# A local transformer on one core: values projected in every step, attention as keys by queries on eight tiles, the output weights gathered in one PSUM bank, and the feed-forward norm folded into W1

## The chip, the core and the metric

The kernel runs on one core of a Trainium2 chip. The core has a matrix engine (PE; its weight loads are listed as PEld), a vector engine (DVE), a scalar engine (ACT), a general engine (POOL) and a queue that issues most DMAs (SP). Each engine works through its own list of instructions in order; semaphores tie the lists together. Matrix products land in PSUM, which has eight banks of 128 partitions by 2 KB. The metric is the device time of one execution in microseconds (us), the median of several runs.

## The reference

All of it is float32. The batch is 16 sequences of 256 tokens, 128 channels. Layer 0 applies a linear-attention block and then a six-layer local transformer; layer 1 applies a causal attention with position bias and a feed-forward block. The change touches the local transformer alone:

```python
# DEPTH 6, HEADS 16, DIM_HEAD 64, WINDOW 32, DIM_INNER 341
for i in range(DEPTH):
    x = attn_layer(shift_tokens(x), Wqkv[i], q_scale[i], k_scale[i], Wo[i]) + x
    x = ffn_layer(shift_tokens(x), ln_g[i], ln_b[i], W1[i], b1[i], W2[i], b2[i]) + x

def attn_layer(x, Wqkv, qs, ksc, Wo):
    q, k, v = heads(x @ Wqkv)
    q, k = rotary(l2norm(q) * qs), rotary(l2norm(k) * ksc)
    # each window of 32 queries sees its own 32 keys and the 32 before
    sim = where(mask, -max, (q @ k_two_windows.T) * 8.0)
    return concat_heads(softmax(sim) @ v_two_windows) @ Wo

def ffn_layer(x, g, bln, W1, b1, W2, b2):
    xn = (x - mean(x)) / sqrt(var(x) + 1e-05) * g + bln
    a, gate = split(xn @ W1 + b1)
    return a * gelu(gate) @ W2 + b2
```

`shift_tokens` takes the second half of the channels from the token before.

## The kernel before

The state is kept channels by tokens, in eight tiles `zs[u]`, one for each unit of 512 tokens (two sequences). The local transformer works layer by layer, unit by unit, and in a unit over four steps; a step `n` handles two pairs of heads, that is four heads. There are 6 x 8 x 4 = 192 steps, and the loop runs 16 more to drain, because a step's work is spread over the iterations after it (lines 1053 to 1137). Iteration `n` does, in the order in which it is written:

- scores, maxima and exponentials of step n-5 (lines 842, 855, 868). The 16 exponentials of an iteration are dealt out between later work by the generator `between`;
- the projection of queries and keys of step n (line 699), four products of 128x128 by 512 columns. ACT squares each bank (703), then DVE multiplies the same bank twice by the rotary tables (706, 709); halves of heads are exchanged by DMA (`sent`, `got`) and added by POOL an iteration later (`rotate`, 719);
- the norms of queries and keys in pairs of steps: sums of squares on PE (727), transposed (745), three Newton steps for the inverse root on POOL (763 to 771), turned into rows (779) which go to DRAM (`home`) and come back spread over partitions as `kn`, with which POOL scales the keys (800);
- the mask for the next scores, copied into PSUM by ACT (828);
- the probabilities of step n-6 are divided by their sums on POOL (889) and transposed in 32x32 blocks by DVE (896) into `prT`;
- attention with merged weights. `upright` (802) transposes the state, and a DMA pair shifts it by one window (`own`, `before`). `weighted` (901, step 910) multiplies the state itself by all 16 heads' probabilities of 128 tokens, in 8 products of 32x128 weights and 512 columns, four banks, copied to `zx` by ACT and DVE (919, 917). `merging` (922, step 927) multiplies that, head by head, by Wv times Wo of that head: 16 products of 128 columns, summed in one bank, and `merged_in` adds them to the state (940). The 16 matrices Wv Wo are made once a layer by `merge_vo` (653 to 680);
- the feed-forward block of a unit, 15 to 19 iterations after the unit's first step: mean by a product (956), square on ACT (961), variance by four one-column products (965), the power -0.5 on POOL (975) and its spreading (977), transposed back (981), the scaling by g and b (982, 983), the gates (990), the values (997), W2 (1007).

The order of PE, DVE, ACT and POOL is the written one (`manual_schedule`); DMA issues on SP are placed by the scheduler. Products land in `bank()`, a pool of five PSUM banks of 128x512; three more hold scores. A bank is handed out again when its last reader has been issued and done; which free bank a product gets goes by the order in which they are released.

Of the kernel before, what the change touches and what calls it, by code (L numbers as in the profile page):

```python
# [19 lines left out]
NU = B // 2  # L20
# [24 lines left out]
def adaln_kernel(  # L45
# [44 lines left out]
    nc.vector.memset(mean128, 1.0 / D)  # L90
    half = cst.tile([128, 16], F32, tag="half", name="half")
# [144 lines left out]
    with block:  # L236
# [17 lines left out]
        centre = wa.tile([128, 128], F32, tag="centre", name="centre")  # L254
        nc.vector.tensor_tensor(centre, ident, mean128, ALU.subtract)
# [342 lines left out]
    with ExitStack() as es:  # L598
        pss = psum(es, 5, 3)
# [26 lines left out]
        own = [persistent(f"own{j}", (128, 4, D)) for j in range(2)]  # L626
        before = [persistent(f"before{j}", (128, 4, D)) for j in range(2)]
# [25 lines left out]
        def merge_vo(i, vo):  # L653

            for g in range(2):
                wv = work("wv")
                c0 = 2 * INNER + g * 512
                nc.sync.dma_start(wv, io["L0_ffn_Wqkv"][i, :, c0 : c0 + 512])
                wo = work("wo").rearrange("p (j d) -> p j d", j=4)
                nc.sync.dma_start(  # L660
                    wo,
                    io["L0_ffn_Wo"][i, g * 512 : (g + 1) * 512, :].rearrange(
                        "(p k) d -> k p d", k=128
                    ),
                )
                yield
                pt = bank()
                for j in range(4):
                    c = slice(j * 128, (j + 1) * 128)
                    nc.tensor.transpose(pt[:, c], wv[:, c], ident)  # L670
                wt = work("wvT")
                nc.scalar.copy(wt, pt)
                yield
                for par in range(2):
                    r = slice(64 * par, 64 * par + 64)
                    pw = bank()
                    for j in range(4):
                        c = slice(j * 128, (j + 1) * 128)
                        nc.tensor.matmul(pw[:, c], wt[r, c], wo[r, j, :], start=True, stop=True)
                    nc.vector.tensor_copy(  # L680
                        vo[:, 8 * g + par : 8 * g + 8 : 2, :],
                        pw.rearrange("p (j d) -> p j d", j=4),
                    )
                yield

        def project(i, u, m, wqk, between):
# [3 lines left out]
            xs = zs[u][:, :, PAD : PAD + L]  # L690
            squares = []
            sent, got = atile("sent", (128, 2, 512)), atile("got", (128, 2, 512))
            q = two(atile("q", (128, 512), 10))
            k = ks[m % 10][:, :, PAD:]
            for j, (name, r) in enumerate((("q", q), ("k", k))):
                tab = [rope[:, j, a].unsqueeze(1).to_broadcast([128, 2, L]) for a in range(2)]
                scale = bcol(i, name + "s")
                pp = bank()
                nc.tensor.matmul(pp, wqk[:, j, :], xs, start=True, stop=True)  # L699
                sq = work("sq")  # L700
                first = False
                if not first:
                    nc.scalar.activation(sq, pp, AF.Square)  # L703
                squares.append(sq)
                next(between, None)
                nc.vector.scalar_tensor_tensor(  # L706
                    two(sent[:, j, :]), two(pp), scale, tab[1], ALU.mult, ALU.mult
                )
                nc.vector.scalar_tensor_tensor(r, two(pp), scale, tab[0], ALU.mult, ALU.mult)  # L709
                if first:  # L710
                    nc.scalar.activation(sq, pp, AF.Square)
# [895 lines left out]
```

## Time and profile before

| | |
|---|---|
| median of 3 runs | 3831.9 us (3828.32 to 3834.38) |
| the profiled execution | 3831.36 us, span 3829.5 us |
| local transformer in it, first projection to last state addition | 264.8 to 3284.6 us |
| PE busy, weight loads, DVE, ACT, POOL, share of the span | 94%, 58%, 74%, 72%, 69% |
| exponentials (L868), 3072 | 1248.7 us, and 755.3 us of accumulator reads |
| projections (L699), 768 products | 730.2 us |
| merging (L927), 3072 products | 718.2 us |
| weighting (L910), 1536 products | 524.6 us |
| scores (L842), 12288 products | 310.6 us |

A float32 product shows as two PE instructions with a weight load each, so the counts in the profile are twice the products. A row of the groups reads: line, engine, operation, output<-input, shapes, count | busy us, mean ns of one | idle time of the engine just before, and what released it. The times of one group overlap on PE, where instructions are pipelined: the mean of one is longer than busy time divided by count. A row of the timeline gives start, length, engine, line and the instructions that stand together.

### The profile page before, as it was taken

To read this page: it belongs to the slowest core of one execution; us is meant where nothing else is said; L and a number is where in the kernel's file an instruction comes from. 1 tells how busy PE (TensorE), PEld (TensorE's weight loads), DVE (VectorE), ACT (ScalarE), POOL (GpSimd) and SP (SyncE) were. 2 spreads that over 40 slices of the span, in tenths; PEclk is the share of its full clock that TensorE was granted. 3 is DMA by queue.
4 is the path that set the end of the run, shared out by engine and by line. 5 is a ranking of instruction groups with operands and counts; after the bars stand their busy time and mean duration, and the time that the engine had idled before them with its cause. 6 is when DMAs were issued, how large, how long until landed. Compare 5 with 4: busy or idle time off the path is not lost.

```text
span 3829.5 us, 120148 instructions
## 1 busy us (share of the span) xinstructions
PE 3597.0 (94%) x46454; PEld 2227.9 (58%) x46454; DVE 2846.2 (74%) x5941; ACT 2768.1 (72%) x9651; POOL 2657.0 (69%) x3380
## 2 busy tenths in 40 slices
PE   7875899999999999999999999999999999789888
PEld 4542566666666666666666666566666666355554
DVE  6745777777777777777777777777777774587774
ACT  4544787878878787777878787787778775366664
POOL 6536877777777777777777777777777772345453
PEclk9887999999999999999999999999999999799998
DMA  1324444544444444454444444444444440201000
GB/s 43 45 61 113 121 112 113 128 108 114 123 109 123 108 115 121 113 125 104 116 121 116 119 113 108 116 119 123 112 110 116 110 106 23 75 16 27 12 21 10
DMA packets 216210, 362.27 MB, mean 95 GB/s; under 512 B 63657, under 2 KB 107608, under 8 KB 215640
## 3 DMA queue, kind: packets, MB, share of 16 engines
q1 hardware_dynamic: 215640, 354.59, 37.6%
q8 instruction: 368, 6.03, 0.7%
q14 instruction: 202, 1.65, 0.1%
HBM read 132.12 MB, written 9.96 MB: 37 GB/s over the span
## 4 chain that ended last, share of the span: by engine, by line
PE 72%; DVE 9%; POOL 8%; ACT 6%; issue 4%; DMA 1%; SPq 1%; POOLq 0%; ACTq 0%; DVEq 0%
PE mm L699 15%; PE mm L927 14%; PE mm L910 9%; PE sim L842 7%; PE mm L727 5%; PE mm L990 3%; PE mm L997 3%; PE mm L1007 3%; POOL k L800 3%; ACT pr L1344 2%; DVE sent L706 2%; PE sim L1315 1%; PE mm L1404 1%; PE mm L956 1%; PE mm L1301 1%
## 5 line engine op out<-in xcount | busy, mean ns | idle before, releaser
L868 ACT ACTIVATE pr<-sim,nb,rq 128x64 f32<-128x64 f32 x3072 | 1248.7, 445 | 19.2 <-DVE nb L859 17.8
L927 PEld LDWEIGHTS mm<-zx,wvo 128*128 128x128 f32 x6144 | 716.5, 192 | 90.6 <-issue 80.3
L868 ACT ACTIVATION_READ_ACCUMULATOR pr<-sim,nb,rq 128x1 f32 x3072 | 755.3, 246 | 0.0
L699 PE MATMUL mm<-z,wqk 128*128 128x512 f32 x1536 | 730.2, 608 | 4.7 <-DMA wqk<-in_L_ffn_Wqkv_dram 4.6
L927 PE MATMUL mm<-zx,wvo 128*128 128x128 f32 x6144 | 718.2, 275 | 1.0 <-DVE zx L917 1.0
L703 ACT ACTIVATE sq<-mm 128x512 f32<-128x512 f32 x768 | 474.5, 618 | 317.5 <-PE mm L699 317.5
L706 DVE SCALAR_TENSOR_TENSOR sent<-mm,vec,rope 128x512 f32<-128x512 f32 x768 | 569.3, 741 | 160.1 <-ACT sq L703 130.8
L889 POOL TENSOR_TENSOR pr<-pr,rsum 128x512 f32<-128x512 f32 x384 | 392.2, 1042 | 419.7 <-DVE rsum L881 414.9
L719 POOL TENSOR_TENSOR q<-q,got 128x512 f32<-128x512 f32 x384 | 496.9, 1294 | 20.0 <-DMA got<-sent 12.5
L800 POOL TENSOR_TENSOR k<-k,kn 128x512 f32<-128x512 f32 x384 | 481.7, 1276 | 14.8 <-DMA kn<-rkh 14.8
L719 POOL TENSOR_TENSOR k<-k,got 128x512 f32<-128x512 f32 x384 | 489.1, 1274 | 0.0
L699 PEld LDWEIGHTS mm<-z,wqk 128*128 128x128 f32 x1536 | 275.7, 192 | 350.5 <-issue 269.6
L855 DVE TENSOR_REDUCE mx<-sim 128x8 f32<-128x512 f32 x384 | 246.6, 683 | 185.9 <-PE sim L842 183.9
L842 PE MATMUL sim<-k,q 64*32 64x64 f32 x24576 | 310.6, 228 | 69.6 <-POOL k L800 55.4
L842 PEld LDWEIGHTS sim<-k,q 64*32 64x32 f32 x24576 | 267.7, 107 | 173.7 <-POOL k L800 114.6
L1358 POOL TENSOR_TENSOR pr<-pr,rsum 128x256 f32<-128x256 f32 (+1 forms) x256 | 206.2, 836 | 221.7 <-DVE rsum L1356 221.5
L1344 ACT ACTIVATE pr<-lg,nm 128x128 f32<-128x128 f32 (+1 forms) x512 | 226.4, 443 | 128.9 <-DVE nm L1333 119.2
L917 DVE COPY zx<-mm 128x512 f32<-128x512 f32 x384 | 247.4, 686 | 67.1 <-PE mm L910 61.3
L709 DVE SCALAR_TENSOR_TENSOR k<-mm,vec,rope 128x512 f32<-128x512 f32 x384 | 284.9, 742 | 0.0
L709 DVE SCALAR_TENSOR_TENSOR q<-mm,vec,rope 128x512 f32<-128x512 f32 x384 | 284.6, 741 | 0.0
L919 ACT COPY zx<-mm 128x512 f32<-128x512 f32 x384 | 210.0, 610 | 99.2 <-PE mm L910 94.2
L910 PE MATMUL mm<-prT,before 32*128 32x512 f32 x1536 | 273.1, 636 | 0.6 <-ACT pr L868 0.6
(250 smaller groups left out, 5832.7 us busy)
## 6 DMA issues: line engine op xcount, KB each, us to landing
got<-sent SPq DMA_DIRECT2D x1536, 128.0 KB
kn<-rkh SPq DMA_DIRECT2D x768, 128.0 KB
before<-own SPq DMA_DIRECT2D x48, 192.0 KB
wqk<-in_L_ffn_Wqkv_dram SPq DMA_DIRECT2D x48, 128.0 KB
v<-vh SPq DMA_DIRECT2D x32, 128.0 KB
bhome<-brow SPq DMA_DIRECT2D x1, 3072.0 KB
wv<-in_L_ffn_Wqkv_dram SPq DMA_DIRECT2D x12, 256.0 KB
wo<-in_L_ffn_Wo_dram SPq DMA_DIRECT2D x12, 256.0 KB
```

What stands on the lines that cost most here:

```text
L699: nc.tensor.matmul(pp, wqk[:, j, :], xs, start=True, stop=True)
L703: nc.scalar.activation(sq, pp, AF.Square)
L706: nc.vector.scalar_tensor_tensor(two(sent[:, j, :]), two(pp), scale, tab[1], ALU.mult, ALU.mult)
L709: nc.vector.scalar_tensor_tensor(r, two(pp), scale, tab[0], ALU.mult, ALU.mult)
L719: nc.gpsimd.tensor_tensor(r, r, two(got[:, j, :]), ALU.add)
L800: nc.gpsimd.tensor_tensor(k, k, two(kn), ALU.mult)
L842: nc.tensor.matmul(sims[par][32 * c : 32 * c + 32, c0 : c0 + 64], q[r, s, t0 : t0 + 32], k[r, s, t0 : t0 + 64], start=False, stop=True, sk ...
L868: nc.scalar.activation(pr[:, x, st, par, :], sims[par][:, b * 64 : (b + 1) * 64], AF.Exp, bias=nb[:, par, b : b + 1], scale=rn[:, par, b : ...
L889: nc.gpsimd.tensor_tensor(prf, prf, rsum[:, x].unsqueeze(2).to_broadcast([128, 8, 64]), ALU.mult)
L910: nc.tensor.matmul(pz[c], xw[b][r, j, :], moving[r, j, b], start=(b == 0), stop=(b == 1))
L927: nc.tensor.matmul(py, vo[:, h, :], zx[:, h % 2, h // 2, :], start=(h == 0), stop=(h == 2 * NP - 1),)
L1344: nc.scalar.activation(pr[:, par, SPANS[t]], lg[:, par, SPANS[t]], AF.Exp, bias=nm[:, t, par : par + 1], scale=-1.0, accum_out=ssum[:, t, ...
```

## The change

- **Values.** `merge_vo`, `upright`, `weighted`, `merging` and `merged_in` go. Each step projects its own four heads' values for the unit (`values`, V0 and V1, one for each sequence): four products with the state as weights and 256 columns of Wv, copied to `v` by ACT.
- **Probabilities.** `pr` is laid out by window first (o=0 the earlier 32 keys, o=1 the own 32). `divided` and `flipped` work on one half at a time (D0, D1, F0, F1). The transposed earlier half goes to `prB` and by two DMAs, shifted by one window, beside the own half in `prT`: so each block of 32 keys stands by the 32 queries of its own window and the 32 of the next one.
- **Attention.** `attended` (A) multiplies, for two head pairs, four token tiles, four key blocks and two heads, 32 keys x 64 channels of `v` by those 64 queries: 64 products on 32x64 tiles, eight different tiles in a row, the four row groups into four banks. `summed` (U) adds what falls to one window: two ACT copies, four DVE additions, into `av`.
- **Output.** `output` (O) multiplies `av` by Wo, two products of 512 columns a step, summed over the unit's four steps in one bank of its own (`psy`); `output_in` (OI) adds it to the state once a unit. The product banks fall from five to four.
- **Feed-forward.** `folded` (ME) puts g into W1, removes the mean from it with the matrix `centre` and puts b into the biases, once a layer. In the unit, the state is transposed (T), DVE's bn_stats and bn_aggr give the variance, and the state times the inverse root (RB) goes straight into W1: the mean product, the square, the variance products and one scaling pass go.
- **Order.** The written loop becomes a list of named steps, `ORDER`. `project` is split into q0, k0, q1, k1, `norms_inverse` into NT and the Newton steps NW. The feed-forward block follows 12 to 15 iterations after a unit's first step, and the drain is 12 iterations.

The names in `ORDER`: T, RB, G, a, W2 the five parts of the feed-forward block; NS, NT, NW, NR the norms (sum, transpose, Newton, rows); S scores, X maxima, E two exponentials at a time, R the inverse sums; RO0, RO1 the additions of the exchanged halves; SC0, SC1 the scaling of the keys; M one mask. A step that has nothing to do in an iteration is skipped: NS, NT, NW come in even iterations, NR in odd ones, T and RB, G, a, W2 in one of four each, OI in one of four.

```diff
-        pss = psum(es, 5, 3)
+        pss = psum(es, 4, 3)
+        psy = es.enter_context(tc.tile_pool(name="psy", bufs=1, space=PSUM))
...
+        def project(i, u, m, wqk, j):
+            name = "qk"[j]
+            if j == 0:
+                sent[m] = atile("sent", (128, 2, 512)), atile("got", (128, 2, 512))
+                qs[m] = two(atile("q", (128, 512), 10))
+                squares[m] = []
+            snd, rcv = sent[m]
+            r = ks[m % 10][:, :, PAD:] if j else qs[m]
+            tab = [rope[:, j, a].unsqueeze(1).to_broadcast([128, 2, L]) for a in range(2)]
+            scale = bcol(i, name + "s")
+            pp = bank()
+            nc.tensor.matmul(pp, wqk[:, j, :], zs[u][:, :, PAD : PAD + L], start=True, stop=True)
+            sq = work("sq")
+            nc.scalar.activation(sq, pp, AF.Square)
+            squares[m].append(sq)
+            nc.vector.scalar_tensor_tensor(
+                two(snd[:, j, :]), two(pp), scale, tab[1], ALU.mult, ALU.mult
+            )
+            nc.vector.scalar_tensor_tensor(r, two(pp), scale, tab[0], ALU.mult, ALU.mult)
+            if j:
+                for c in range(0, 128, 64):
+                    nc.sync.dma_start(rcv[c : c + 32], snd[c + 32 : c + 64])
+                    nc.sync.dma_start(rcv[c + 32 : c + 64], snd[c : c + 32])
+                got[m] = rcv
+                del sent[m]
...
+        def divided(pr, rsum, o):
+            prf = pr[:, o].rearrange("p t x h k -> p (t x h) k")
+            nc.gpsimd.tensor_tensor(
+                prf, prf, rsum.unsqueeze(2).to_broadcast([128, 16, 32]), ALU.mult
+            )
+        def flipped(pr, prT, o):
+            late = prT[:, 0] if o else atile("prB", (128, 4, 128))
+            nc.vector.transpose(
+                late.rearrange("p t n -> p (t n)"), pr[:, o].rearrange("p t x h k -> p (t x h k)")
+            )
+            if o == 0:
+                nc.sync.dma_start(prT[0 : 128 - WIN, 1], late[WIN:128])
+                nc.sync.dma_start(prT[128 - WIN : 128, 1, 0:4:2], late[0:WIN, 1:4:2])
+        def values(v, u, wv, h):
+            pv = bank()
+            for t in range(2):
+                c = PAD + 128 * t
+                nc.tensor.matmul(
+                    pv[:, t * 256 : (t + 1) * 256],
+                    zs[u][:, h, c : c + 128],
+                    wv,
+                    start=True,
+                    stop=True,
+                )
+            nc.scalar.copy(v[:, 2 * h : 2 * h + 2].rearrange("p t c -> p (t c)"), pv)
...
+        def attended(prT, v):
+            pa = [bank() for _ in range(4)]
             for x in range(2):
...
+                for t in range(4):
+                    for c in range(4):
+                        r = slice(WIN * c, WIN * c + WIN)
+                        n = 1 if t % 2 and c == 3 else 2
+                        for par in range(2):
+                            c0 = (2 * x + par) * 32
+                            o0 = (4 * x + t) * 64
+                            nc.tensor.matmul(
+                                pa[c][64 * par : 64 * par + 64, o0 : o0 + 32 * n],
+                                v[r, t, 2 * c0 : 2 * c0 + 64],
+                                prT[r, 0:n, t, c0 : c0 + 32],
+                                start=True,
+                                stop=True,
+                                skip_group_check=True,
+                            )
+            return pa
...
+        def summed(pa):
+            av = atile("av", (128, 8, 6, 32))
+            p = [b.rearrange("p (n o q) -> p n o q", n=8, o=2) for b in pa]
+            nc.scalar.copy(av[:, :, 0:5:4], p[0])
+            nc.scalar.copy(av[:, :, 2:6:3], p[2])
+            for c, old in ((1, 4), (3, 5)):
+                nc.vector.tensor_tensor(av[:, :, c], p[c][:, :, 0], av[:, :, old], ALU.add)
+            nc.vector.tensor_tensor(av[:, :, 2], p[1][:, :, 1], av[:, :, 2], ALU.add)
+            nc.vector.tensor_tensor(
+                av[:, 1:8:2, 0], p[3][:, 0:8:2, 1], av[:, 1:8:2, 0], ALU.add
+            )
+            return av
+        def output(av, wo, j):
+            if j == 0:
+                outs.append(psy.tile([128, 512], F32, tag="psy", name="psy"))
+            for x in range(2):
                 nc.tensor.matmul(
...
+                    outs[-1].rearrange("p (t n) -> p t n", t=4),
+                    wo[:, x, :],
+                    av[:, 4 * x : 4 * x + 4, 0:4].rearrange("p t c q -> p t (c q)"),
+                    start=(j == 0 and x == 0),
+                    stop=(j == QS - 1 and x == 1),
+                )
+        def output_in(u, py):
             for hf in range(2):
                 r, zv = zpart(u, hf)
...
+                nc.vector.tensor_tensor(zv, two(py)[r], zv, ALU.add)
...
+        def folded(i):
+            w1 = wffs[i][0]
+            fb = small("fb", (128, 2, 3), 2)
+            raw = vec[:, _B_BASE + i * len(_B_VECS) + _B_COL["a0"] :][:, 0:6].rearrange(
+                "p (j c) -> p j c", j=2
+            )
+            pb = bank()
+            for j in range(2):
+                for c, n in enumerate(FFC):
+                    c0 = j * FFH + c * 128
+                    nc.tensor.matmul(
+                        pb[0:n, 3 * j + c : 3 * j + c + 1],
+                        w1[:, c0 : c0 + n],
+                        bcol(i, "b"),
+                        start=True,
+                        stop=True,
+                    )
+            pb = pb[:, 0:6].rearrange("p (j c) -> p j c", j=2)
+            nc.vector.tensor_tensor(fb[:, :, 0:2], pb[:, :, 0:2], raw[:, :, 0:2], ALU.add)
+            r = slice(0, FFC[2])
+            nc.vector.tensor_tensor(fb[r, :, 2], pb[r, :, 2], raw[r, :, 2], ALU.add)
+            biases[i] = fb
+            nc.gpsimd.tensor_scalar(w1, w1, bcol(i, "g"), None, ALU.mult)
+            yield
+            for j in range(2):
+                pw = bank()
+                c = slice(j * FFH, (j + 1) * FFH)
+                nc.tensor.matmul(pw[:, 0:FFH], centre, w1[:, c], start=True, stop=True)
+                nc.vector.tensor_copy(w1[:, c], pw[:, 0:FFH])
...
         def ffn(u, i):
             src = zs[u][:, :, PAD : PAD + L]
-            pm = bank()
-            nc.tensor.matmul(pm, mean128, src, start=True, stop=True)
-            xn = ftile("fx")
-            nc.vector.tensor_tensor(two(xn), src, two(pm), ALU.subtract)
-            yield
-            sq = ftile("fs")
-            nc.scalar.activation(sq, xn, AF.Square)
-            yield
-            pv = bank()
+            pt = bank()
             for t in range(4):
-                nc.tensor.matmul(
-                    pv[:, t : t + 1],
-                    sq[:, t * 128 : (t + 1) * 128],
-                    mean128[:, 0:1],
-                    start=True,
-                    stop=True,
-                )
+                s, c = t // 2, PAD + 128 * (t % 2)
+                nc.tensor.transpose(
+                    pt[:, t * 128 : (t + 1) * 128], zs[u][:, s, c : c + 128], ident
+                )
+            st = small("st", (128, 4, 6), 2)
+            mv = small("mv", (128, 4, 2), 2)
+            for t in range(4):
+                nc.vector.bn_stats(st[:, t, :], pt[:, t * 128 : (t + 1) * 128])
+            for t in range(4):
+                nc.vector.bn_aggr(mv[:, t, :], st[:, t, :])
             ve = small("ve", (128, 4))
-            nc.vector.tensor_scalar(ve, pv[:, 0:4], 1e-5, None, ALU.add)
+            nc.vector.tensor_scalar(ve, mv[:, :, 1], 1e-5, None, ALU.add)
...
-            nc.vector.tensor_tensor(xn, xn, rb, ALU.mult)
-            nc.vector.tensor_scalar(xn, xn, bcol(i, "g"), bcol(i, "b"), ALU.mult, ALU.add)
+            xn = ftile("fx")
+            nc.vector.tensor_tensor(two(xn), src, two(rb), ALU.mult)
...
+        ORDER = (
+            "T E NS E S E E X R A D0 D1 O U E E RO0 SC0 F0 OI NT q0 E k0 q1 W2 F1 M "
+            "E RB V0 M SC1 V1 RO1 ME NR G NW a k1 "
+        ).split()
+        n = 0
+        while n < N + 12:
+            layer, at_ = divmod(n, per)
+            if at_ == 11 and 0 < layer < DEPTH:
+                wffs[layer] = load_ffn(layer)
+            if at_ == (11 if layer else 3) and layer < DEPTH:
+                merges.append(folded(layer))
+            for name in ORDER:
+                STEP[name](n)
+            prs.pop(n - 6, None)
+            next_layer(n, load_qks, wqks)
+            next_layer(n - 6, load_v, wvs)
+            next_layer(n - 8, load_o, wos)
             n += 1
         stage["flat"] = None
...
```

## The prediction

> **What bounds the kernel now.** First the page's busy line, then the windows, which show where the time lies:
>
> ```profile
> PE 3597.0 (94%) x46454; PEld 2227.9 (58%) x46454; DVE 2846.2 (74%) x5941; ACT 2768.1 (72%) x9651; POOL 2657.0 (69%) x3380
> ```
>
> ```profile
> 400.00:1600.00 1200.00, 1185.20 (x16173) 742.17 (x16172) 941.00 (x1651) 952.29 (x3366) 936.13 (x1197) 1.00 0.47 117
> 3140.00:3240.00 100.00, 90.90 (x1192) 61.90 (x1191) 51.21 (x96) 63.82 (x236) 41.40 (x48) 0.98 0.14 38
> ```
>
> Columns: window, length, busy PE, PEld, DVE, ACT, POOL, granted clock, DMA share, GB/s. In the local transformer (264.8 to 3284.6 us) PE is busy 98.8% at full clock; DVE, ACT and POOL stand at 78 to 79%. So PE's work sets the rate, and each of the others has about 3 us of slack in a 15 us step. The chain that ended last passes the same eight projections once per unit (four steps), which gives the period:
>
> ```profile
> 1041.44 3.63 PE mm L699 x8
> 1104.14 3.63 PE mm L699 x8
> ...
> 1650.24 3.63 PE mm L699 x8
> 1710.68 3.63 PE mm L699 x8
> 1771.09 3.63 PE mm L699 x8
> ```
>
> 60.4 us a unit; 62.7 where `merge_vo` falls in (+2.3 a layer). PE's timeline prices the parts, start to next start:
>
> ```profile
> 1708.58 0.86 PE L842 MATMUL sim<-k,q 64*32 64x64 f32 x64
> 1709.82 0.86 PE L842 MATMUL sim<-k,q 64*32 64x64 f32 x64 [0.39 <-POOL k L800]
> 1710.61 3.70 PE L699 MATMUL mm<-z,wqk 128*128 128x512 f32 x8
> 1714.15 3.73 PE L927 MATMUL mm<-zx,wvo 128*128 128x128 f32 x32
> 1717.81 1.43 PE L910 MATMUL mm<-prT,before 32*128 32x512 f32 x8
> 1718.77 1.32 PE L910 MATMUL mm<-prT,own 32*128 32x512 f32 x8
> 1720.03 2.84 PE L990 MATMUL mm<-fx,w 128*128 128x512 f32 x6
> 1722.70 0.27 PE L779 MATMUL mm<-ident,rk 128*32 128x128 f32 x1
> 1722.91 1.48 PE L842 MATMUL sim<-k,q 64*32 64x64 f32 x128
> ```
>
> Merging costs 3.67, weighting 2.2 (2.0 in calmer steps), four projections 3.54 (0.885 each), scores 1.41 to 1.66. Last the groups that price what is new:
>
> ```profile
> L842 PE MATMUL sim<-k,q 64*32 64x64 f32 x24576 | 310.6, 228 | 69.6 <-POOL k L800 55.4 <-ACT sim L828 7.7 <-issue 6.3
> L1382 PE MATMUL mm<-prT,v 32*64 32x128 f32 x4608 | 97.5, 283 | 1.4 <-issue 0.8 <-DVE q L1303 0.6
> L706 DVE SCALAR_TENSOR_TENSOR sent<-mm,vec,rope 128x512 f32<-128x512 f32 x768 | 569.3, 741 | 160.1 <-ACT sq L703 130.8 <-DMA kn<-rkh 19.6 <-DMA rope<-in_c_rope_dram 5.0
> ```
>
> L842 is a product on eight tiles with 64 moving columns; L1382 uses the tile shape of the new attention with 128. L706 shows that DVE's rope multiplication follows ACT's square of the same bank: a projection's bank is held by two engines in turn.
>
> **PE, part by part.** Removed per unit: merging 4x3.67=14.7, weighting 4x2.1=8.4, the norm's mean product 0.96 and its variance columns 0.91 (L956, L965), `upright` 0.61: 25.6. Added per unit:
> - Values (V0, V1), four products of 256 columns a step. Between 0.229 for 128 columns (L927, two instructions) and 0.885 for 512 a line gives 0.448: 1.79 a step, 7.2.
> - Output (O), two products of 512 columns: 1.77 a step, 7.1.
> - The transposes T: 0.61, as `upright`'s.
> - Attended (A), 64 products, 128 load and multiply pairs a step. No row has this shape. Low end 1.41, the fastest scores (64 moving columns, 32 weight columns). High end: 144 pairs of L1382 take 2.62 without the last one's latency, 18.2 ns a pair, so 2.33. I take 1.6, by the scores, whose moving width and count it shares: 6.4; both ends are kept.
>
> Added 21.3. The rows of the old unit add up to 59.7 against 60.4 measured; with the same 0.7 unlisted, the new unit is 60.4-25.6+21.3=56.1 of PE work.
>
> *A rule against it.* The Trainium skill, "TensorE: Matmul & The Clock Gate", section "LDWEIGHTS (loading the stationary operand)", prices a load by its columns over 1.2 GHz: 53 ns for 64. In series, 128 loads would be 6.8 us a step and the kernel some 1000 us slower. The L1382 row, 18 ns a pair although one load alone shows 135, speaks for overlap between tiles, and I go by the row.
>
> **What the new order makes PE wait for.** The banks for products fall from five to four (one is kept for the gathered output), and A takes all four. I walk an odd step from t=0, the end of k1 on PE. ACT squares k1's bank to 0.65; DVE's two multiplications (1.31 a pair, from L706 and L709 back to back) hold it to 2.05. PE's scores end at 1.55, so A runs 2.2 to 3.8: 0.6 of waiting. In even steps NS (1.85) lies between, and there is none. After A, ACT copies p0 and p2 (done at 4.45 and 4.95) and DVE adds p1 and p3 (three additions of 256 columns at 0.40 and one of 128 at 0.27, from a 64x128 addition of 0.271 and a 128x512 one of 0.688; done at 6.1). Output covers PE to 5.6; q0 and k0 find p0's and p2's banks free. DVE then does F0 (0.62) and three pairs, from 7.1 to 11.05. PE has done q0, k0, q1, V0, V1 and NR by 10.2 and wants V0's bank (ACT, 10.6) and q1's (11.05) for the gates: 0.5 in the step with G. In the step with W2, k1 waits 0.2 for the state's additions. Sum 2x0.6+0.5+0.2=1.9 a unit; bounds 0 (as now, 1% idle) and 6.4 (0.6 at A and 1.0 later in each step). New unit 58.0, 2.4 less than now: 48x2.4=-115.
>
> **Off PE, costed at nothing:**
> - ACT: two copies of p0, p2 (about 0.5 each back to back) added, zx's two replaced by V's, `upright`'s and the norm's square gone: 12.0 to 12.7 of a 14.5 step. The exponentials now write runs of 32; a copy with such runs took 610 ns (L919), one without 589 (L811): at most 0.2 a step more, none if not. Cover gone, it would delay U and with it q0.
> - DVE: zx copies (1.29) and `merged_in` (0.56) a step go; U is 1.5, OI and W2 lie once a unit: 12.0 stays 12.0. bn_stats and bn_aggr have no row: the four pairs lie between 1.1 (208 ns for a 16-column operation, 83 for an accumulator read) and 2.2 (349 for 128 columns from PSUM, 208), against two removed passes of 0.63; taken even. T's step has NS, so X is not late by them.
> - POOL: a scaling of W1 a layer more (682 columns, some 1.4 by 256 in 556 ns, L1255); else unchanged, but NW (4.6, L763 to L771) stands last in even steps and spills some 6 us into the next: D0 comes 2 later there, F0 and three rope pairs behind it 0.8. That lies within the bounds of the waits.
> - SP: two shift DMAs of prT a step more, 14.5 for 12.5, at 0.6 each some 9 of 14.5. The first waits for F0; k0's exchange queues behind it and is due a step later. Two transfers per unit (`before`) go, and a layer's weights come in 8 loads of 128 KB for V and Wo, not 4 of 256; they are issued a layer ahead, as the queries' are. A reads the shifted half a step later, about 8 us after issue.
>
> **Edges.** `folded` in place of `merge_vo`: 12 one-column instructions at 0.114 (L965) and 4 of 341 columns at 0.31: 2.6, with a bank wait 3.1 against 2.3: +5 in six layers. The drain from the last projection took 143, of which the unit's sum counts 118; with three steps less of lag some 92 of 75: 25 idle becomes 17. Filling waits for the first keys either way: -5 in all (bounds -20 and +10).
>
> **Sum.** The profiled execution took 3831.4 (span 3829.5 and 1.9 around it), 0.5 under the median. 3831.4-115+5-5=3716; by the median 3717.
>
> **Rivals.**
> 1. PE stays full, the four banks suffice. For it: ACT, DVE and POOL keep 2 us a step of slack. Against: k1's bank in odd steps. 56.1 a unit, 48x4.3=-206: 3625.
> 2. The tiles run as in the last stage (L1382), 2.33 for 1.6: +0.73x192=+140: 3857, slower by 0.7%; at half that distance 3787. For it: the same weight tiles. Against: half the moving columns.
> 3. Slower: the loop k1, square, rope, A, U, q0 becomes the bound. Place: A and U, where all four banks are held. Price: 0.6 at A plus 1.0 before the next product in every step, 6.4 a unit, 62.5: +2.1x48=+101: 3933. It decides from 4.3 us of waiting a unit, 1.1 a step. For it: DVE waits 130.8 us on ACT's squares already, with five banks. Against: Output and the values give PE work that needs no late bank.
>
> **How the numbers follow.** Forecast 0.38 (own range 3660 to 3770), rival 1 0.23, rival 2 0.16 (half of it still faster), rival 3 0.21, anything else 0.02. Faster by over 0.2% (7.7 us, about what a measurement of this kernel tells from none): 0.38+0.23+0.10=0.71; within 0.04; slower 0.25. The range 3600 to 3880 takes in rival 1, the high price of the tiles, and the near part of rival 3.
>
> **What would show it.** A unit's period of 58 in the chain; the attended line with 128 pairs in 1.5 to 1.8 us; PE at 95 to 97% in the steady window, idle before attended (released by DVE) and before the gate product. Wrong if the attended run takes over 2 us, if PE idles over 1 us a step, or if ACT exceeds 90%.

## The result and the profile after

The changed kernel took 4156.7 us (median of 4 runs, 4141.2 to 4171.2) against 3831.2 for the kernel before on the same chip: a ratio of 1.085, with a 95% interval of 1.081 to 1.089. It is slower by 325 us; 3717 had been forecast, and even the price of rival 3, 3933, was passed by 224. The profiled execution took 4156.6 us, its span 4154.8.

The busy line of the page after, and further down the row of DMA queue 8, which the page calls "instruction" (packets, MB, share):

```profile
PE 3575.6 (86%) x63494; PEld 2066.3 (50%) x63494; DVE 2843.9 (68%) x6517; ACT 2925.6 (70%) x9929; POOL 2657.7 (64%) x3382
...
q8 instruction: 501, 8.21, 0.9%
```

The same queue before:

```profile
q8 instruction: 368, 6.03, 0.7%
```

PE has less busy time than before (3576 for 3597 us), yet it is busy for 86% of the span and no longer for 94%. No other engine has filled up: ACT, the fullest, stands at 70%. PE has 17,040 more products and as many more loads; queue 8 will matter below. The window that showed 1185.20 us of PE and a clock of 1.00 before now reads:

```profile
400.00:1600.00 1200.00, 1052.40 (x20527) 600.50 (x20526) 830.07 (x1671) 895.12 (x3054) 825.25 (x1054) 0.95 0.44 113
```

PE stands still for 148 us of 1200, and the granted clock (third column from the right) has fallen to 0.95. The chain of waits, whose W2 product comes once a unit, gives the new period:

```profile
1582.15 2.58 PE mm L1035 x6
...
1649.62 2.58 PE mm L1035 x6
...
1718.07 2.58 PE mm L1035 x6
...
1930.62 2.58 PE mm L1035 x6
```

From the first line to the last it is five units (two more W2 products lie where the fence leaves out), 69.7 us each, where 60.4 had been and 58.0 was forecast. These five are a little slower than most: over all units between 400 and 3140 us the trace gives 68.9 each, against 60.7 before. PE's timeline shows where PE stands (start, length, line, instructions; in brackets the idle time before and what ended it):

```profile
2008.67 1.76 PE L813 MATMUL sim<-k,q 64*32 64x64 f32 x128
2010.36 1.47 PE L898 MATMUL mm<-prT,v 32*64 32x64 f32 x107
2013.96 0.42 PE L898 MATMUL mm<-prT,v 32*64 32x64 f32 x21 [2.13 <-issue]
2014.31 2.65 PE L928 MATMUL psy<-av,wo 128*128 128x512 f32 x4
...
2024.71 1.62 PE L813 MATMUL sim<-k,q 64*32 64x64 f32 x128
2026.26 0.36 PE L898 MATMUL mm<-prT,v 32*64 32x64 f32 x12
2026.95 0.90 PE L898 MATMUL mm<-prT,v 32*64 32x64 f32 x64 [0.34 <-issue]
2029.12 1.07 PE L898 MATMUL mm<-prT,v 32*64 32x64 f32 x52 [1.27 <-issue]
2030.12 3.18 PE L928 MATMUL psy<-av,wo 128*128 128x512 f32 x4
...
2043.98 1.74 PE L813 MATMUL sim<-k,q 64*32 64x64 f32 x128
2045.65 0.47 PE L898 MATMUL mm<-prT,v 32*64 32x64 f32 x31
2048.23 1.30 PE L898 MATMUL mm<-prT,v 32*64 32x32 f32 x97 [2.11 <-issue]
2049.47 3.66 PE L928 MATMUL psy<-av,wo 128*128 128x512 f32 x4
```

Attended (L898) starts as soon as the scores (L813) are through, and then breaks off in the middle of its 128 pairs, after 107, after 76, after 31: a different place each time, while the loop does the same in every step. No tile or bank of the step changes hands at pair 107 or 31. The wait is called "issue": the profile shows nothing that PE waited for. The short stop after exactly 12 is another thing, although it too is called "issue": pair 13 is the first that needs the fourth bank. It occurs in 70 of the 192 steps, 33 us in all, and in 65 of the 70 it ends within 0.6 us (0.1 in most) behind DVE's multiplication L691 on the bank of k1. Output (L928), which takes 1.98 us where it stands undisturbed (first experiment below), takes 2.65 to 3.66 behind such a stop, a part of it or all at half the clock. From 400 to 3300 us, PE's longest wait and its two at the scores, and first one of POOL that will matter (us in total, times, longest):

```profile
POOL k L786 <- DMA kn<-rkh: 313.7, 103, 11.0
...
PE mm L898 <- issue: 283.7, 218, 2.9
...
PE sim L813 <- issue: 14.3, 17, 1.2
...
PE sim L813 <- POOL k L786: 7.6, 6, 2.2
```

What is short is PE's own instructions. Three readings of the trace's records say so. First, queue 8 carries PE's program: its packets are 16,384 bytes, and the trace has 128,234 records of PE (products, loads, semaphores), which by the 501 packets is 256.0 each; before it is 256.0 too, by 368. Second, that queue has a packet from 2011.0 to 2012.5 on the timeline above; PE stops at 2011.8 and goes on at 2014.0. There are 206 stops in the middle of a group that end 0.9 to 1.7 us after the end of a packet, and within these bounds they lie close together: 1.37 us is the median, nine in ten are between 1.23 and 1.53. A packet itself takes 0.9 to 1.6. Third, between one such stop of over 0.6 us and the next lies a multiple of 256 of these records, 512 or 768 mostly, in 165 cases of 165 (from 400 to 3300 us). Counted from the trace's first record, all 183 of these stops in the whole stage stand at the same remainder by 256, and it is the same remainder in all 187 of the run below with the scores issued twice: PE stops at a packet's border. From a packet's start to its first instruction's execution it thus takes some 2.3 to 2.9 us, and scores with attended use up two packets in 3.1. Behind the long stops the packet had started only 1.3 us (median) after PE entered the 256 instructions before, so a group of 256 that runs through in 1.5 us is over before the next packet can be used.

The table counts this in each kernel's trace for the stage of the local transformer, here from the first projection to the last product: PE's idle stretches over 0.15 us that end 0.9 to 1.7 us behind a packet of instructions, in the middle of a group ("short of instructions"); all other such idle stretches; and the time lost to the clock, the sum of time by (1 - granted). The last runs on through idle time too, so the columns overlap somewhat.

| us | stage | short of instructions (stops) | other stops | clock |
|---|---|---|---|---|
| before | 3018 | 7 (10) | 87 | 46 |
| after | 3350 | 310 (206) | 108 | 191 |

The stage grew by 332: +303 short of instructions, +145 clock, +21 other stops; the rest, -137, is work that PE was spared (a high bound of it, by the overlap). The clock's loss belongs to the stops: 92 of its 98 stretches at half the clock, 172 us of the 191, lie at a stop that was short of instructions.

The Trainium skill, "Runtime: NRT & Kernel Launch", section "Instruction fetch mechanics", says that instructions come in blocks of 16 KiB, 256 instructions, and that the cost of crossing a block's border is mostly hidden. The blocks agree with these packets; that the crossing is hidden holds for the kernel before (7 us) and not for this one (310).

### The profile page after: what moved, and what is told of

Read it like the earlier page. It is cut to its first block, busy times and chain, and to the rows that moved or that the text cites. A ratio compares the mean times of both kernels' runs of the same rounds, so it can differ in the third digit from the quotient of the medians.

```text
span 4154.8 us, 155191 instructions
## 1 busy us (share of the span) xinstructions
PE 3575.6 (86%) x63494; PEld 2066.3 (50%) x63494; DVE 2843.9 (68%) x6517; ACT 2925.6 (70%) x9929; POOL 2657.7 (64%) x3382
## 4 chain that ended last, share of the span: by engine, by line
PE 62%; issue 11%; ACT 8%; DVE 5%; POOL 3%; DMA 3%; SPq 2%; POOLq 0%; ACTq 0%; DVEq 0%
PE mm L684 11%; PE psy L928 10%; PE mm L898 8%; PE sim L813 7%; PE mm L877 5%; PE mm L709 4%; PE mm L1025 3%; PE mm L1035 3%; PE mm L1018 3%; ACT pr L1437 2%; ACT sq L686 2%; ACT pr L839 2%; DMA kn<-rkh 2%; PE sim L1408 1%; PE mm L1497 1%
## 5 line engine op out<-in xcount | busy, mean ns | idle before, releaser
L839 ACT ACTIVATE pr<-sim,nb,rq 128x64 f32<-128x64 f32 x3072 | 1210.7, 418 | 1.1 <-DVE nb L830 0.5
L686 ACT ACTIVATE sq<-mm 128x512 f32<-128x512 f32 x768 | 439.0, 601 | 420.7 <-PE mm L684 412.0
L839 ACT ACTIVATION_READ_ACCUMULATOR pr<-sim,nb,rq 128x1 f32 x3072 | 670.9, 218 | 0.0
L898 PE MATMUL mm<-prT,v 32*64 32x64 f32 (+1 forms) x24576 | 380.6, 235 | 317.4 <-issue 315.7
L928 PE MATMUL psy<-av,wo 128*128 128x512 f32 x768 | 509.3, 798 | 8.6 <-issue 8.6
L898 PEld LDWEIGHTS mm<-prT,v 32*64 32x64 f32 x24576 | 325.8, 133 | 369.3 <-issue 346.2
L916 DVE TENSOR_TENSOR av<-mm,av 128x256 f32<-128x256 f32 x384 | 163.2, 425 | 366.5 <-ACT av L913 319.9
L877 PE MATMUL mm<-wv,z 128*128 128x256 f32 x1536 | 380.5, 385 | 16.1 <-DVE k L691 9.7
L813 PEld LDWEIGHTS sim<-k,q 64*32 64x32 f32 x24576 | 272.7, 105 | 202.4 <-issue 111.0
L877 PEld LDWEIGHTS mm<-wv,z 128*128 128x128 f32 x1536 | 284.8, 191 | 144.0 <-issue 74.3
L813 PE MATMUL sim<-k,q 64*32 64x64 f32 x24576 | 313.8, 226 | 41.4 <-POOL k L786 26.3
L913 ACT COPY av<-mm 128x512 f32<-128x512 f32 x192 | 112.6, 587 | 281.4 <-PE mm L898 277.7
```

Of the source, the lines that this page charges most:

```text
L813: nc.tensor.matmul(sims[par][32 * c : 32 * c + 32, c0 : c0 + 64], q[r, s, t0 : t0 + 32], k[r, s, t0 : t0 + 64], start=False, stop=True, sk ...
L839: nc.scalar.activation(pr[:, :, st, x, par, :], sims[par][:, b * 64 : (b + 1) * 64].rearrange("p (o k) -> p o k", o=2), AF.Exp, bias=nb[:, ...
L877: nc.tensor.matmul(pv[:, t * 256 : (t + 1) * 256], zs[u][:, h, c : c + 128], wv, start=True, stop=True,)
L898: nc.tensor.matmul(pa[c][64 * par : 64 * par + 64, o0 : o0 + 32 * n], v[r, t, 2 * c0 : 2 * c0 + 64], prT[r, 0:n, t, c0 : c0 + 32], start=True,
L928: nc.tensor.matmul(outs[-1].rearrange("p (t n) -> p t n", t=4), wo[:, x, :], av[:, 4 * x : 4 * x + 4, 0:4].rearrange("p t c q -> p t (c q) ...
```

## The experiments

Two theories. **Instructions**: two groups of 256 small instructions in direct succession, scores and attended, outrun the supply; the stops and the half clock behind them are the loss. **Banks** (the prediction's own waits, grown): attended takes all four banks, and stops because one of them is late. A third, that the mere number of PE's instructions decides, is told apart from the first by the two runs with the small products apart from the scores.

### Output between scores and attended

```diff
-            "T E NS E S E E X R A D0 D1 O U E E RO0 SC0 F0 OI NT q0 E k0 q1 W2 F1 M "
+            "T E NS E S E E X R O A D0 D1 U E E RO0 SC0 F0 OI NT q0 E k0 q1 W2 F1 M "
```

> The step order alone differs from the changed kernel: output (O) stands between scores (S) and attended (A), so that 512 short PE instructions no longer follow each other. Theory 1 (PE's instruction supply): PE uses 256 instructions of S and 256 of A in 3 us, new blocks of 256 arrive too slowly, PE stands about 2 us inside A and its clock is halved afterwards. Then the idle time put down to issue before attended falls from 316 us to under 100, output costs about 1.9 us a step again and not 2.65, and the time falls to 3850 to 4020 (a new wait of up to 0.8 us a step for summed's banks is in this). Theory 2 (the four banks that A takes make PE wait): only k1's bank gains, summed loses its cover; the idle time before attended stays over 250 us and the time is 4130 to 4250.

Measured: 3959.0 us, 1.033 [1.030, 1.035] of before; 198 us of the 325 are gone by moving two products of a step. PE's timeline of this run:

```profile
2033.30 1.73 PE L813 MATMUL sim<-k,q 64*32 64x64 f32 x128
2034.96 1.98 PE L928 MATMUL psy<-av,wo 128*128 128x512 f32 x4
2036.87 1.68 PE L898 MATMUL mm<-prT,v 32*64 32x64 f32 x128
2039.15 0.66 PE L727 MATMUL mm<-ident,n 128*128 128x128 f32 x4 [0.60 <-ACT av L913]
```

and its waits:

```profile
PE mm L898 <- issue: 49.5, 78, 2.9
PE mm L727 <- ACT av L913: 49.5, 83, 0.7
PE mm L877 <- DVE q L691: 49.4, 100, 1.2
```

With 1.9 us of wide products in between, attended runs through in 1.68, near the price of 1.6 that was forecast for it; it does so without a stop in 111 of 192 steps. Stops for instructions fall from 310 to 70 us, the clock's loss from 191 to 34. In exchange the cover that output gave is gone: the next products stand 0.6 for ACT's copies of attended's banks. So the banks do hold PE up, once the instructions don't; the single stop has the size that the prediction's walk gives (p0's copy is done 0.65 behind attended).

### The kernel before with the scores issued twice

```diff
-                scores(sims, m, [qs.pop(m), qs.pop(m + 1)])
+                pair = [qs.pop(m), qs.pop(m + 1)]
+                scores(sims, m, pair)
+                scores(sims, m, pair)
```

> The kernel before with the 64 score products of a step issued twice in a row, the second set added to the first (so it attends with doubled scores, which is not what the reference computes). No bank, wait or DMA is added; 512 short PE instructions follow each other as in the changed kernel. Theory 1 (instruction supply): the work adds 192 times 1.5 = 288 us, and stalls of about 2 us inside the scores with a halved clock after them come on top: 4350 to 4700, with over 150 us of issue idle before the scores' products. Theory 2 (banks): the work alone: 4080 to 4150.

Measured: 4564.1 us, 1.191 [1.188, 1.193]. This kernel has five banks, no values, no attended and the old order; it has only 128 more small pairs behind the 128 of the scores, so that the scores count double. Its timeline and its longest wait on PE:

```profile
2016.16 2.92 PE L842 MATMUL sim<-k,q 64*32 64x64 f32 x255
2021.55 0.21 PE L842 MATMUL sim<-k,q 64*32 64x64 f32 x1 [2.48 <-issue]
...
2023.47 4.48 PE L699 MATMUL mm<-z,wqk 128*128 128x512 f32 x8
```

```profile
PE sim L842 <- issue: 330.3, 173, 3.6
```

A single pair comes 2.48 us late, and the eight products of the projection behind it take 4.48 for 3.70. 362 us are lost to instructions in 197 stops, and 120 more than before to the clock. The banks have no part in this.

### The same small products, apart from the scores

The same 64 products a step, now of zeros into the two banks that the mask was just copied to; first ahead of merging, then behind it:

```diff
+        def nothing_added(sims):
+            for x in range(2):
+                for st in range(4):
+                    for c in range(4):
+                        for par in range(2):
+                            r = slice(64 * par, 64 * par + 64)
+                            c0 = x * 256 + st * 64
+                            nc.tensor.matmul(
+                                sims[par][32 * c : 32 * c + 32, c0 : c0 + 64],
+                                nought[r, :],
+                                rope[r, 0, 0, 0:64],
...
+            if 0 <= n - 4 < N:
+                nothing_added(banks[-2:])
             w, j = divmod(n - 11, QS)
             if 0 <= w < DEPTH * NU:
                 py = merging(zxs.pop((w, j)), vos[w // NU])
```

> The kernel before with as many small products added as in the run with the scores issued twice (64 a step, the same tile form, 64*32 by 32x64, into the same two banks), but apart from the scores: they add a stationary of zeros to the two freshly masked banks of the next step, between the wide products of the second projection and those of merging, so that no 256 of PE's instructions in 1.5 us directly follow another 256. If the pauses come from small products in direct succession outrunning PE's instruction supply (theory), this costs the products' own time, 192 steps of 1.5 us, 288 us at most, so 4000 to 4150 us, and the pauses of the small products inside their group stay under 60 us in all. If it is the number of PE's instructions alone that costs (rival), the time is that of the doubled scores, 4500 to 4600 us, with some 200 pauses and 350 us. If the wide products, and not the small ones, are slowed by any more work on PE (a lower clock for load's sake), the granted clock of the stage falls below 0.93 with no pauses.

Measured: 5027.0 us, 1.311 [1.307, 1.315]: neither theory's time. Its longest wait on PE tells why:

```profile
PE sim L861 <- ACT sim L830: 456.1, 227, 3.9
```

The added products stand up to 3.9 us for the copy of the mask (612 us over the stage, in 300 stops), and the clock, halved behind such stops, loses 437 us. Short of instructions it was for 30 us. The expectation's third case, a low granted clock with no pauses, is not it either: the clock is low (0.90 over the span), but the pauses are long. The place was badly chosen, and the run says nothing clean on the theories. So the call was moved behind merging, which covers the copy:

> As the run before (the 64 products of zeros a step, added to the two banks of the next step), now issued one step of the order later, between merging and weighting instead of ahead of merging: there PE had stood 2 to 3 us a step for the copy of the mask, and merging, 3.7 us of wide products, now covers that copy. The small products have merging's 32 pairs in 3.7 us ahead of them and weighting's 16 in 2 us behind them, then the scores. Theory (direct succession of two groups of 256 instructions outruns the supply): only the products' own time, up to 288 us, so 4050 to 4180 us, pauses inside small groups under 80 us, granted clock of the span about as before (0.96). Rival (the number of PE's instructions alone decides): as with doubled scores, 4500 to 4600 us, about 200 pauses, 350 us.

Measured: 4118.2 us, 1.074 [1.070, 1.077]: 282 us over before, where 192 steps of 1.5 us are 288. The timeline and the waits of PE in this run:

```profile
2010.10 3.73 PE L946 MATMUL mm<-zx,wvo 128*128 128x128 f32 x32
2013.76 1.66 PE L861 MATMUL sim<-rope,nought 64*32 64x64 f32 x128
2015.35 1.14 PE L929 MATMUL mm<-prT,before 32*128 32x512 f32 x8
...
2017.28 2.84 PE L1016 MATMUL mm<-fx,w 128*128 128x512 f32 x6
2020.05 1.59 PE L844 MATMUL sim<-k,q 64*32 64x64 f32 x128
```

```profile
PE sim L861 <- ACT sim L830: 26.5, 75, 2.8
PE sim L844 <- issue: 7.9, 8, 2.2
```

This kernel draws more packets of instructions in its stage (502 in 3312 us) than the changed one (445 in 3350) and loses 12 us to them, not 310. Its clock loses 37 us, no more than before, so more products do not lower the clock by themselves. The number of instructions alone is not it; their succession is: as many small products of the same form cost 282 us apart (of zeros, here) and 730 back to back.

### Output split, half ahead of attended and half behind

```diff
-            "T E NS E S E E X R A D0 D1 O U E E RO0 SC0 F0 OI NT q0 E k0 q1 W2 F1 M "
+            "T E NS E S E E X R O0 A D0 D1 O1 U E E RO0 SC0 F0 OI NT q0 E k0 q1 W2 F1 M "
```

> The changed kernel with the first of the two output products between scores and attended and the second behind attended. Instruction supply: 0.9 us of wide work between the two runs instead of 0 (changed kernel, 310 us of instruction gaps) or 1.8 (e1_output_between, 70 us): 100 to 180 us of gaps. The second product covers the copy of the first bank, so the waits of NT and q0 for it (110 us in e1_output_between) shrink to under 40. 3900 to 4000.

Measured: 3946.9 us, 1.030 [1.028, 1.031], the lowest of the changed kernel's variants, though not clear of the run with all of output between (1.030 to 1.035).

```profile
PE mm L898 <- issue: 151.2, 156, 2.4
```

With one product in between, 180 us of stops are left, but shorter ones (median 0.9 us for 1.5), and the clock loses 63 us, not 191. The second half of output covers ACT's copies again, and the other stops fall to 126 from the 238 of the run with all of output ahead.

### Three more orders

Values (V0, V1) between scores and attended, output split; the feed-forward transposes and the sums of squares (T, NS) between them, output split; and scores moved behind q1, with 12 buffers of queries and keys for 10:

```diff
+            "T NS E S E V0 E V1 E X R O0 A D0 D1 O1 U E E RO0 SC0 F0 OI NT q0 E k0 q1 W2 F1 M "
+            "E RB M SC1 RO1 ME NR G NW a k1 "
```

> As e6_output_split, with the values products (V0, V1) also between scores and attended, so that 2.7 us of wide products lie between the two runs of short ones, and V0 and V1 no longer behind q1, whose bank they waited for. Instruction supply: gaps fall from 180 us to under 70, clock loss to the 46 us of the kernel before, waits on banks stay under 120: 3770 to 3850. If the gaps stay over 120 us, the distance between the runs is not what decides; if the gaps fall and the time stays over 3900, the waits of the other engines came back.

```diff
+            "E S E E E X T NS R O0 A D0 D1 O1 U E E RO0 SC0 F0 OI NT q0 E k0 q1 W2 F1 M "
```

> As e6_output_split, with T and the norm sums (NS, 1.85 us in every second step) moved from ahead of the scores to behind them, ahead of attended; the four exponentials stand ahead of the maxima. Instruction supply: the gaps vanish in even steps alone, so about half of 180 us stays: 80 to 120 us, clock loss 45 to 60; 3850 to 3920.

```diff
+            "T NS E O A E U E R D0 D1 OI NT RO0 F0 q0 SC0 k0 F1 q1 S X W2 E RB SC1 k1 "
+            "E M V0 E V1 RO1 ME E M NR G NW a E "
```

> The changed kernel with another step order: output, attended and summed at the start of a step, the scores and maxima only after q1, the two values products at its end; queries and keys have 12 buffers instead of 10, which the later scores need. The two runs of short products are then 4 us or more of wide products apart on both sides. Instruction supply: idle time of PE inside attended and scores under 60 us, clock loss as in the kernel before (46 us); the scores cover the wait of the values for q1's bank (61 us in e1_output_between). 3800 to 3900. If the waits on banks come back elsewhere, because DVE and ACT now have their maxima and exponentials in the middle of the projections, 3900 or more with under 100 us of instruction gaps.

Measured: 4114.3 us (1.072 [1.069, 1.075]), 4011.5 (1.046 [1.044, 1.048]) and 4934.0 (1.287 [1.285, 1.289]): all three slower than forecast. The stops for instructions fell in each against the changed kernel (126, 149 and 30 us), but with the values between and with the norms between by less than expected (under 70, and 80 to 120). For the values between, over 120 was to mean that the distance between the two small groups is not what decides, and 2.7 us of wide products did leave more stops than the 1.9 of the first experiment (70). By the trace the packet itself comes late there: behind the stops of over 0.6 us it had started 3.7 us (median) after PE entered the 256 instructions before, and not 1.3. What starts a packet no run shows, so a distance that suffices cannot be given. Besides, the order of the other engines hangs on the same list. The long waits off PE, first with the values between, then with the scores apart:

```profile
DVE rsum L852 <- ACT pr L839: 349.0, 165, 3.5
POOL pr L857 <- DMA kn<-rkh: 306.0, 45, 12.0
```

```profile
ACT pr L839 <- DVE nb L830: 784.6, 137, 6.5
POOL pr L857 <- DVE nx L729: 711.4, 69, 15.1
```

In the last, the exponentials stand right behind the maxima and wait for them, and PE's other stops come to 914 us. An order that spares PE's supply alone is not yet a good order.

### Half of the scores

The scores of the second head pair are left out, so its probabilities come from the mask alone.

```diff
-            for x in range(2):
+            for x in range(1):
                 q, k = qs[x], ks[(m + x) % 10]
```

> The changed kernel with the score products of the first of the two head pairs only (the second pair's probabilities are those of the mask, not of the reference): 128 short PE instructions less before attended, all else the same. Theory 1 (instruction supply): 192 times 0.75 = 145 us of work less, and more than half of the 316 us of issue idle and of the clock loss (131 us over the kernel before) gone too: 3700 to 3850. Theory 2 (banks): the scores cover k1's bank, so the wait takes most of the work's place: 4010 to 4157.

Measured: 4218.8 us, 1.101 [1.096, 1.105]: less work, and slower than both theories said. The stops for instructions fell as expected, to 118 us, but other stops rose to 461, and the clock's loss, which was to fall, to some 270:

```profile
POOL k L786 <- DMA kn<-rkh: 640.3, 133, 11.4
DVE prB L865 <- POOL pr L857: 377.4, 86, 8.8
PE mm L877 <- DVE q L691: 173.4, 65, 5.9
```

The scheduler places the issues on SP anew in every kernel. Here `kn`'s stand behind the new shift DMAs of `prT`, which wait for F0, and behind the exchange; POOL waits for `kn`, D0 behind it is late, then F0 on DVE, then DVE's part of the projection, whose bank the values need. In the changed kernel the same wait of POOL is 314 us in the view above, where it was 3.5 before; there PE's scores wait for POOL no longer than before (7.6 us, 24.4 before); that PE's own stops cover the wait is argued, not shown.

### The folded norm alone, in the kernel before

```diff
-            pm = bank()
-            nc.tensor.matmul(pm, mean128, src, start=True, stop=True)
...
+            for t in range(4):
+                nc.vector.bn_stats(st[:, t, :], pt[:, t * 128 : (t + 1) * 128])
...
+            if at_ == (14 if layer else 3) and layer < DEPTH:
+                merges.append(folded(layer))
```

> The feed-forward part of the change alone, in the kernel before: bn_stats, W1 with g and the mean removed, five parts instead of seven. By the prediction's rows PE saves 0.96+0.91-0.61 = 1.3 us a unit (60 us) and pays about 3 us a layer (18 us): 3780 to 3800. Theory 1 has nothing against it, since no short products are added. If the folded norm was a cause of the loss, 3830 or more.

Measured: 3834.7 us, 1.000 [0.999, 1.001]. PE's busy time did fall, by 23 us (3573.9), and went into new waits of PE:

```profile
PE mm L966 <- DMA w<-in_L_ffn_W_dram: 18.6, 5, 4.2
PE mm L1038 <- DVE z L942: 9.2, 42, 0.2
```

`folded`'s first product (L966) waits for its weights once a layer, and W2's first product in a unit (L1038) for an addition to the state (L942), which by the code can only be for the bank that the addition reads. The expectation called 3830 or more a sign that the folded norm is a cause of the loss; but the time is that of the kernel before, so the saving failed to come and nothing was lost. This part of the change neither harms nor helps where it was put here; the loss lies in the other part.

## Why the prediction was wrong, point by point

**The step that failed** is the reading "PE's work sets the rate", from which each added product was priced by its own duration and summed. It took PE's instructions as always at hand, and the clock as full. Neither the number of instructions nor what stands next to what was looked at, though the page of before had a row for the instruction queue, and the diff put 256 small instructions directly behind 256 others. The two omitted terms are +303 and +145 us of the stage.

**Attended, taken at 1.6 with bounds 1.41 and 2.33:** near. Where it runs through, with output between, it takes 1.68 at the median (1.59 to 1.91 for eight in ten). So rival 2 (slow tiles, 2.33) is out. In the changed kernel itself the run took 3.7 with its stops (median), so the sign "over 2 us" came true as well, by the stops and not by the tiles.

**The waits for four banks, 1.9 us a unit, 91 in all:** the mechanism is there, the size smaller as long as instructions are short. The forecast stop of attended for k1's bank is the one after 12 pairs, 0.34 in the timeline above for the 0.6 worked out; all stops of PE that were not for instructions grew by 21 us together. In the run with output between, where the supply is better, they are 238 us: 151 more than before, and more than the 91. Its new waits for `av` name the place of rival 3 (attended, U, the next product). But in the changed kernel rival 3's loop is not the bound; that the time ended on its side is no merit of it.

**PE's work, 4.3 us a unit less (206):** less than that came. The account gives 137 as a high bound; in the run with output between, where the overlap of the columns is small, it gives 75. The folded part alone spared 23 us of busy time for about 42 that its terms make (48 x 1.26 less six layers of 3.1). Most of the rest is price: in the run with output between, from start to next start at full clock, values took 8.1 us a unit for the 7.2 of the prediction's line between two widths, output 7.7 for 7.1, attended 7.1 for 6.4, which is 2.1 us a unit or 101 in all; the projections and scores, which did not change, took 0.8 us a unit more than before.

**"Off PE, costed at nothing":** in the changed kernel these engines held PE up little, and ACT ended at 70%; but PE was slower than forecast, so this is luck and no test of the terms. The term for SP was wrong in its queue: `kn` also stands behind the shift DMAs, not the exchange alone, and POOL waits 314 us for it. With half of the scores that wait reaches PE, by the chain of rows shown there; with the values between POOL's wait for `kn` is as long (306 us), and how much of it reaches PE was not followed up.

**Rival 1** (PE full, 3625) is out by the window: 88% busy, where the forecast itself had 95 to 97. The sign by which the prediction was to be known wrong, PE idle over 1 us a step, came true (310 us in 192 steps). The idle time before attended was to be released by DVE; most of it is "issue", in its middle.

**What stays open.** No variant of the changed order got back to before: the best lies at 1.030. Whether an order exists that separates the two small groups and keeps the other engines' cover was not found out. What decides when a packet is started, and so how close two small groups may stand, was not found out.

## What to carry to other kernels

Count PE's instructions as well as their time: in a float32 kernel each product is two products and two loads, and where a change puts one run of small products (256 instructions in 1.5 us) directly behind another, ask whether the supply follows; a stop called "issue" at changing places within a group is the sign, and two wide products in between are a first remedy (198 us of the 325 here). Price a stop of PE with the clock behind it, not by its length alone. And when steps of a written order are moved for one engine's sake, go through what stands on the other engines' lists, and on the DMA queue, before the next run.

## What the runs showed of the hardware

- In these runs PE's stops for instructions stand at the borders of 16 KB packets of its program, 256 instructions each, and end 1.37 us (median of 206; 1.23 to 1.53 for nine in ten) after a packet's end; a packet takes 0.9 to 1.6. 256 instructions in 1.5 us twice in a row cost 1.5 us of idle time (median of 206 stops in 192 steps, 310 us); with 1.9 us of wide products in between 70 us were left, with wide products on both sides of each small group 12.
- The clock fell to half behind pauses of some 2 us: behind 2.1 us of idle time, output took 3.66 for 1.98 us, and the clock's records show 0.5 for 3.4 us or a multiple of it at a time. It did so at 29 of the 48 stops of 1.9 to 2.3 us, and at none of the 22 under 0.6. The Trainium skill, "TensorE: Matmul & The Clock Gate", section "Why this matters for your kernels", names idle gaps of over about 3 us; here some 2 us were enough.
- Of what the pauses cost in the changed kernel, the clock was about a third: 145 us beside 303.
